# Expert rows that carry token number and residual: results scattered to token order, and a last stage that reads rows in order

## The chip, the cores and the metric

The kernel runs on one core of one Trainium2 chip. The metric is the device time of one execution in microseconds (us), as the median of several runs. The engines are named as in the profile: PE is TensorE (matrix products and transposes), DVE is VectorE, ACT is ScalarE, POOL is GpSimd, and SP is SyncE, which only issues DMAs here. A name with a q behind it (SPq, ACTq, POOLq) is an engine's own instruction queue. An indirect DMA takes the row addresses of one side from a column of integers in SBUF; POOL issues all of them.

## The reference, cut to what matters

The input is x, four images of 256 channels and 48 x 48 pixels, in float32. There are two layers. Each has a mixing part on the images and a feed-forward part (FFN) on tokens; a token is one pixel with its 256 channels. The change touches what happens from the end of layer 1's mixing part on.

```python
# layer 0: dynamic 7x7 attention, then an FFN on each image's 1151 tokens of highest router weight
x = x + attention0(_ln_c(x))
t = _to_tokens(x)
t = t + _L0_ffn_ref(_ln_t(t), ...)
x = _from_tokens(t, x)
# layer 1: four convolutions with weights of +-1, then a switch of 8 experts
x = x + convs1(_ln_c(x))
t = _to_tokens(x)
t = t + _L1_ffn_ref(_ln_t(t), ...)
x = _from_tokens(t, x)

def _L1_ffn_ref(h, gate_w, gate_b, w1, b1, w2, b2):     # T = 9216 tokens, E = 8 experts
    C = math.ceil(1.25 * T / E)                         # 1440 slots of each expert
    probs = softmax(x @ gate_w + gate_b)
    idx = argmax(probs);  prb = probs[idx]
    pos = cumulative count of idx's expert, in token order, minus 1
    kept = pos < C
    buf[idx, pos] = x                                   # tokens past the capacity are dropped
    ybuf = relu(buf @ w1 + b1) @ w2 + b2                # by expert
    y = ybuf[idx, min(pos, C - 1)] * (prb * kept)
    return nan_to_num(y, nan=0, posinf=10000, neginf=-10000)
```

Every token has at most one slot of one expert. The result of that slot, times the gate's probability, is added to the token's residual, which is t ahead of the layer norm. The output has the channels in front, so the last thing that the kernel does is to transpose tokens.

## The kernel before, in words

The kernel is written for a tile framework. A tile pool gives each named tile a number of buffers (`bufs`); an instruction that writes a tile waits until the former users of that buffer are done. The framework places each instruction on its engine's queue, and every queue runs in order. DMAs of SP and ACT share eight completion lanes and those of POOL have eight others; a DMA is issued only when the former DMA of its lane has landed.

There are four stages, and in the profile they follow one another with some overlap.

**Stage 1** (function body from line 162) is layer 0's attention. `conv` (L264) convolves four output rows of each of the four parity images with 49 taps, `attend` makes the softmax over the taps, which goes to DRAM in skewed form and back (`skew<-sp`, L313, and `at<-skew`, L315, both on SP), and `mix` adds the result and writes rows of tokens to the DRAM buffers `xl`. At its start ACT's queue issues 14 loads of the convolution's weights (L185). DVE and POOL make the batch norm's factors; one step is a power on POOL (L198). A tile of zeros (L218, L219) is written 40 times by SP (L383) over the whole of `xbuf`, so that empty slots of the experts read as zeros. `rank_count` counts, on DVE, how many tokens precede each one by router weight, and POOL scatters the token numbers by rank (`order<-ids`, L155).

**Stage 2** runs two things beside each other. `fetch` and `ffn` gather the chosen tokens' rows by indirect DMA (`g<-xl`, L454), apply layer 0's FFN and scatter the rows back (`xl<-y`, L492). The other is a software pipeline over 24 groups of 384 tokens (L640 to L657): `load` (`xt<-xl`) and norm, `to_channels`, `conv1` (L524), `to_tokens`, `gate` and `place`, each one step behind the former. `to_tokens` transposes the convolution's result back (L539), adds it to the residual, which stays in the resident tile `xt3` (L541), and writes the norm of it into a tile `row` of 128 x 3 x 260 with three buffers. `gate` puts the probability into column 256 of `row`. `place` works out each token's slot, keeps the slot in `gslot` and the mark of a kept token in `kept`, both resident, and scatters the three 128-row parts of `row` to their slots in the DRAM buffer `xbuf` (L618). Tokens without a slot get a number past the end and are not written.

**Stage 3** has 24 passes: eight experts with three passes each of 480 slots. `gather` loads the slots' rows from `xbuf` in one DMA (three buffers). `expert` transposes them (L695), makes the hidden layer (L702) and the output (L710), adds the bias and multiplies by the gate (L712, L713), applies nan_to_num to the whole tile (L721 to L724) and writes it to the same slots of the DRAM buffer `ybuf` (L725). ACT's queue loads the next expert's weights.

**Stage 4** has a loop over the same 24 groups. POOL gathers each 128 tokens' rows from `ybuf` by `gslot` (L757), DVE multiplies them by the mark and adds the residual of `xt3` (L760), PE transposes (L763), ACT and DVE copy the two halves of the channels (L766) into a tile `o` with two buffers, and SP writes it to the output (L768).

What the changed lines wait for can't be read from a loop alone. In stage 2 the buffer of `row` comes free when the three scatters of the group three steps back have landed. In stage 4 the gathers of `ybuf` wait for the last write of it.

Of the kernel before, what the change touches and what calls it, by code (L numbers as in the profile page):

```python
# [8 lines left out]
F32 = mybir.dt.float32  # L9
# [9 lines left out]
HW = H * W  # 2304 tokens of an image  # L19
NT = HW // P  # 18 tiles of 128 tokens  # L20
NG = 6  # groups of 8 image rows
GT = 384  # tokens of a group
KA = 49  # attention taps
SELK = 1151  # tokens that layer 0's FFN processes: top_k's first k - 1
NSEL = 9  # tiles of 128 ranks that hold them
E, CAP = 8, 1440  # experts, and the slots of each
FF = 1024
NF = FF // P
XROW = 260  # a row of the experts' buffer: 256 channels, the gate, padding
HOFF = [-4, -2, -1, 0, 1, 2, 4]  # offsets of layer 1's convolutions  # L30
FMAX = 3.4028234663852886e38

# One image, by row and column parity, is four 24x24 images in which the 7x7
# convolution and the attention have no dilation. They are padded to 30x30.
SP = 30
SRC = 10 * SP  # source pixels of four output rows
PITCH = 306  # a row of the attention matrix in DRAM; skewed writes use PITCH + 1
# [3 lines left out]
def metaformer_kernel(ctx: ExitStack, tc: tile.TileContext, i, out):  # L41
# [18 lines left out]
    # before[p, j] = j < p; after[p, j] = j > p; upto[p, j] = p <= j  # L60
# [13 lines left out]
    # 1 for every rank but the last of the ninth tile  # L74
# [3 lines left out]
    ids = const.tile([P, NT], I32, tag="ids", name="ids")  # L78
    nc.gpsimd.iota(ids, pattern=[[P, NT]], base=0, channel_multiplier=1)

# [14 lines left out]
    # rows of layer 0: [x + LN(x) | LN(x)], by image  # L95
    xl = [dram.tile([HW, 2 * C], F32, tag=f"xl{b}", name=f"xl{b}") for b in range(B)]
    # token of each rank, by image
    order = [dram.tile([HW, 1], I32, tag=f"order{b}", name=f"order{b}") for b in range(B)]
    xbuf = dram.tile([E * CAP, XROW], F32, tag="xbuf", name="xbuf")
    ybuf = dram.tile([E * CAP, C], F32, tag="ybuf", name="ybuf")  # L100

    def token_norm(work, src, dst, eps, np_=P):
        """dst = LN(src) over the free dim of [np_, 256]."""
# [9 lines left out]
    # Ranks of an image's router weights, ties by the lower token, are counted three tiles at  # L113
    # a time beside the next image's convolution.
# [4 lines left out]
    # the first tile has no earlier tokens, the last no later ones  # L119
# [42 lines left out]
    with ExitStack() as s1:  # L162
# [198 lines left out]
        for s in range(B * NG + 1):  # L361
# [20 lines left out]
            for k in range(2 * s, min(2 * s + 2, 40)):  # L382
                nc.sync.dma_start(zrows[k], zero)  # L383
# [10 lines left out]
    with ExitStack() as s2:  # L394
# [245 lines left out]
        for s in range(-1, len(groups) + 5):  # L640
# [3 lines left out]
            if c := now[0]:  # L644
                normed[c] = load(*c)
# [167 lines left out]
```

## Time and profile before

| What | Before |
|---|---|
| Median of three runs | 3820.05 us |
| Lowest and highest | 3817.47 and 3824.94 us |
| Span of the profiled execution | 3814.3 us |
| PE busy | 3545.5 us, 93% |
| DVE, ACT and POOL busy | 1211.3, 434.0 and 480.0 us |
| All DMA queues | 174.36 MB, 46 GB/s on average |
| Last expert result to the end of the span | 3708.0 to 3814.3, 106.3 us |

The span runs from the first to the last instruction that the profiler records in one execution, and the page gives no other time for that execution. The median of the runs shown is 5.75 us longer than the span.

A row of a group names the line, engine, operation and tiles (written<-read), then the number of instructions, the busy time, the mean time of one in nanoseconds, and the idle time of the engine ahead of them with what ended it. A row of waits has the engine, the instruction that waited, what it waited for, the sum, the number of waits and the longest. A row of DMA issues ends with the median time from issue to landing. In the rows of 40 slices each slice is 95.4 us long and a digit is the busy share in tenths; PEclk is the granted clock of TensorE in tenths. A row of the timeline has the start, the duration and the instruction, and in brackets how long its engine had been idle and what released it.

### The profile page before, as it was taken

The numbers are of one execution on the slowest core, as the hardware profiler recorded it, in microseconds if no ns is written. First come the engines' busy times: TensorE is split into PE (matmuls) and PEld (weight loads), VectorE is DVE, ScalarE is ACT, GpSimd is POOL, SyncE is SP. The second block draws the span as 40 slices with busy tenths as digits, with TensorE's granted clock in tenths as the row PEclk, the third lists the DMA queues.
The fourth block names the chain that finished last, engine by engine and source line by source line (L and its number), as shares of the span: only waits on it lengthen the run. The fifth ranks groups of instructions, "written<-read, shape, count | busy, mean of one in ns | idle before, by whom it ended". The sixth has DMA issues, their size and how long they took to land. (4 is left out here: it accounts for less than half of the span.)

```text
span 3814.3 us, 32485 instructions
## 1 busy us (share of the span) xinstructions
PE 3545.5 (93%) x12832; PEld 2248.8 (59%) x12832; DVE 1211.3 (32%) x3618; ACT 434.0 (11%) x779; POOL 480.0 (13%) x774
## 2 busy tenths in 40 slices
PE   6999999999999999999994789999999499999985
PEld 3566666666666666666663556666565366666652
DVE  3012124312235112261116312333443243333434
ACT  1001000000100000100001111211010022121211
POOL 1000001100001000020002322232332100000006
PEclk9999999999999999999996889999999699999995
DMA  7001100001100000110002221111000222222106
GB/s 231 13 25 39 36 25 25 25 25 35 40 25 25 25 25 27 34 27 21 21 21 76 62 63 31 41 34 44 18 17 18 80 61 59 59 62 66 49 27 193
DMA packets 122840, 174.36 MB, mean 46 GB/s; under 512 B 17089, under 2 KB 96193, under 8 KB 122689
## 3 DMA queue, kind: packets, MB, share of 16 engines
q1 hardware_dynamic: 92800, 111.41, 10.4%
q0 software_dynamic: 13824, 33.23, 2.9%
q10 hardware_dynamic: 16064, 27.66, 2.2%
q8 instruction: 100, 1.64, 0.2%
q14 instruction: 52, 0.42, 0.0%
HBM read 91.69 MB, written 80.58 MB: 45 GB/s over the span
## 5 line engine op out<-in xcount | busy, mean ns | idle before, releaser
L264 PE MATMUL c<-xp,cw 128*128 128x384 f32 x4704 | 1568.5, 492 | 0.9 <-DVE xp L256 0.9
L264 PEld LDWEIGHTS c<-xp,cw 128*128 128x128 f32 x4704 | 885.0, 189 | 663.0 <-issue 304.1
L524 PE MATMUL pc<-xq,cw 128*128 128x384 f32 x1344 | 467.1, 501 | 0.0
L329 DVE COPY av<-pa 120x192 f32<-120x192 f32 x96 | 32.0, 358 | 1096.9 <-PE pa L327 1096.9
L524 PEld LDWEIGHTS pc<-xq,cw 128*128 128x128 f32 x1344 | 254.8, 195 | 164.6 <-issue 12.8
L710 PE MATMUL pey<-ew,ehid 128*120 128x256 f32 x1536 | 335.4, 379 | 0.0
L702 PE MATMUL peh<-xeT,ew 128*128 128x480 f32 x768 | 316.5, 571 | 3.1 <-ACT xeT L697 3.1
L710 PEld LDWEIGHTS pey<-ew,ehid 128*120 128x120 f32 x1536 | 281.1, 183 | 59.2 <-issue 10.4
L109 POOL TENSOR_SCALAR bnrs<-bnmv 128x1 f32<-128x1 f32 x216 | 47.1, 223 | 1865.3 <-DVE bnmv L108 1864.0
L702 PEld LDWEIGHTS peh<-xeT,ew 128*128 128x128 f32 x768 | 145.0, 191 | 159.7 <-issue 151.0
L337 PE MATMUL pv<-av,xt 120*128 120x96 f32 (+1 forms) x1152 | 226.6, 329 | 0.0
L337 PEld LDWEIGHTS pv<-av,xt 120*128 120x128 f32 (+1 forms) x1152 | 181.8, 214 | 39.3 <-issue 11.4
L712 DVE TENSOR_TENSOR ey<-pey,eb 120x256 f32<-120x256 f32 x96 | 40.7, 424 | 431.1 <-PE pey L710 431.1
L269 ACT ACTIVATE k<-c,cb 128x384 f32<-128x384 f32 x24 | 14.0, 583 | 1323.4 <-PE c L264 1266.1
L757 POOL DMA_INDIRECT yt<-ybuf,gslot x72 | 69.9, 971 | 720.8 <-DMA ybuf<-ey 699.1
L704 ACT ACTIVATE ehid<-peh,eb 128x480 f32<-128x480 f32 x192 | 127.0, 662 | 294.6 <-PE peh L702 293.2
L480 PE MATMUL ph<-gt,fw 128*128 128x384 f32 x384 | 137.8, 520 | 6.2 <-ACT gt L475 5.8
L486 PE MATMUL py<-fw,hid 128*128 128x256 f32 x576 | 126.8, 379 | 3.0 <-DVE y L489 3.0
L110 POOL TENSOR_TENSOR bnrs<-bnrs,mhalf 128x1 f32<-128x1 f32 x216 | 125.0, 583 | 13.3
L486 PEld LDWEIGHTS py<-fw,hid 128*128 128x128 f32 x576 | 109.3, 190 | 21.1 <-DVE y L489 3.8
L480 PEld LDWEIGHTS ph<-gt,fw 128*128 128x128 f32 x384 | 76.7, 203 | 63.6 <-ACT gt L475 9.5
L763 PE MATMUL po<-ident,yt 128*128 128x128 f32 x144 | 50.8, 448 | 57.2 <-DVE yt L760 56.1
(169 smaller groups left out, 2599.3 us busy)
## 6 DMA issues: line engine op xcount, KB each, us to landing
xl<-rows SPq DMA_DIRECT2D x24, 768.0 KB, 3.5
ew<-in_L_ffn_w_dram ACTq DMA_DIRECT2D x16, 1024.0 KB, 5.4
skew<-sp SPq DMA_DIRECT2D x24, 575.6 KB, 4.3
at<-skew SPq DMA_DIRECT2D x24, 562.5 KB, 4.8
xbuf<-zero SPq DMA_DIRECT2D x40, 292.5 KB, 7.8
xe<-xbuf SPq DMA_DIRECT2D x24, 487.5 KB, 4.5
ybuf<-ey SPq DMA_DIRECT2D x24, 480.0 KB, 3.6
x<-in_x_dram SPq DMA_DIRECT2D x24, 384.0 KB, 3.4
```

The source lines that it names most:

```text
L109: nc.gpsimd.tensor_scalar_add(rs[:np_], mv[:np_, 1:2], eps)
L110: nc.gpsimd.tensor_tensor(rs[:np_], rs[:np_], mhalf[:np_, 0:1], ALU.pow)
L264: nc.tensor.matmul(ps, lhsT=cw1[:, cc, t, :], rhs=xp[:, cc, :, 4 * g + ki:4 * g + ki + 4, kj:kj + 24], start=(t == 0 and cc == 0), stop=(t ...
L337: nc.tensor.matmul(pv[:, q], lhsT=xts[b, g + k][:n, q, cc * P:(cc + 1) * P], rhs=av[:n, q, k], start=(k == 0), stop=(k == 2))
L480: nc.tensor.matmul(ph, lhsT=fw1[:, cc, f * P:(f + 1) * P], rhs=gt[:, cc], start=(cc == 0), stop=(cc == 1))
L486: nc.tensor.matmul(py, lhsT=hid[:, f, k * P:(k + 1) * P], rhs=fw2[:, f], start=(f == 0), stop=(f == NF - 1))
L524: nc.tensor.matmul(ps, lhsT=cws[n][:, cc, t], rhs=xq[:, cc, 4 + 8 * g + dy:12 + 8 * g + dy, 4 + dx:4 + dx + W], start=(t == 0 and cc == 0) ...
L702: nc.tensor.matmul(ph, lhsT=w1[:, cc, f * P:(f + 1) * P], rhs=xeT[:, cc], start=(cc == 0), stop=(cc == 1))
L704: nc.scalar.activation(hid[:, f], ph, AF.Relu, bias=eb1[:, e * NF + f:e * NF + f + 1])
L710: nc.tensor.matmul(py[:R], lhsT=hid[:, f, j * R:(j + 1) * R], rhs=w2[:, f], start=(f == 0), stop=(f == NF - 1))
L757: nc.gpsimd.indirect_dma_start(out=y, out_offset=None, in_=ybuf, in_offset=bass.IndirectOffsetOnAxis(ap=gslot[b][:, n:n + 1], axis=0))
L763: nc.tensor.transpose(pts[cc][:, k * P:(k + 1) * P], y[:, cc * P:(cc + 1) * P], ident)
```

## The change

A row of `xbuf` becomes 516 elements wide: 256 of the norm, the gate, the token's number as an integer, two of padding, and 256 of the residual. `ybuf`, `xt3`, `gslot` and the resident `kept` go. A new DRAM buffer `fin` has one row of 256 for each token.

- In stage 1 the zero tile covers two rows of 516 per partition; its token column holds `NONE`, a number past the end. It is written 45 times.
- In stage 2 the residual's tile is a work tile `x` with five buffers. `to_tokens` adds the convolution and the residual into the last 256 columns of `row`, writes the token numbers with a POOL copy, and SP writes the residual of all 384 tokens to their rows of `fin`. `place` loses two small DVE operations.
- In stage 3 each of the four 120-row parts of a pass gets its residual added on DVE, and is scattered by POOL to the token rows of `fin`. Empty slots carry `NONE` and are not written. The order of the DMAs on `fin` is kept by the framework.
- In stage 4 ACT's queue loads the 384 rows of a group from `fin` in order; there is no gather and no addition. The loop over the halves of the channels is now outside that over the three parts, and `o` has three buffers.

```diff
-XROW = 260  # a row of the experts' buffer: 256 channels, the gate, padding
+XHEAD = 260
+XROW = XHEAD + C
+NONE = 1 << 30
...
-    ids = const.tile([P, NT], I32, tag="ids", name="ids")
+    ids = const.tile([P, B * NT], I32, tag="ids", name="ids")
...
-    ybuf = dram.tile([E * CAP, C], F32, tag="ybuf", name="ybuf")
+    fin = dram.tile([B * HW, C], F32, tag="fin", name="fin")
...
-        zero = wpool.tile([P, 585], F32, tag="zero", name="zero")
-        nc.gpsimd.memset(zero, 0.0)
-        zrows = xbuf.rearrange("n r -> (n r)").rearrange("(k p r) -> k p r", p=P, r=585)
+        zero = wpool.tile([P, 2, XROW], F32, tag="zero", name="zero")
+        nc.gpsimd.memset(zero.rearrange("p j r -> p (j r)"), 0.0)
+        nc.gpsimd.memset(zero[:, :, C + 1:C + 2].bitcast(I32), NONE)
+        zrows = xbuf.rearrange("(k p j) r -> k p j r", p=P, j=2)
...
-            for k in range(2 * s, min(2 * s + 2, 40)):
+            for k in range(2 * s, min(2 * s + 2, 45)):
                 nc.sync.dma_start(zrows[k], zero)
-    xpool = pool("xtok", 1)
-    xt3 = [xpool.tile([P, NT, C], F32, tag=f"xt3_{b}", name=f"xt3_{b}") for b in range(B)]
-    gslot = [xpool.tile([P, NT], I32, tag=f"gslot{b}", name=f"gslot{b}") for b in range(B)]
-    kept = [xpool.tile([P, NT], F32, tag=f"kept{b}", name=f"kept{b}") for b in range(B)]
...
-            x = xt3[b][:, 3 * g:3 * g + 3]
+            x = work.tile([P, 3, C], F32, tag="x", name=f"x1_{b}_{g}", bufs=5)
...
-            x = xt3[b][:, 3 * g:3 * g + 3]
             row = work.tile([P, 3, XROW], F32, tag="row", name=f"row{b}_{g}", bufs=3)
-            nc.gpsimd.memset(row[:, :, C + 1:], 0.0)
+            nc.gpsimd.memset(row[:, :, C + 2:XHEAD], 0.0)
+            nc.gpsimd.tensor_copy(
+                row[:, :, C + 1].bitcast(I32), ids[:, b * NT + 3 * g:b * NT + 3 * g + 3])
...
-                nc.vector.tensor_add(x[:, k], pt, x[:, k])
-                token_norm(work, x[:, k], row[:, k, :C], 1e-5)
+                xk = row[:, k, XHEAD:]
+                nc.vector.tensor_add(xk, pt, x[:, k])
+                token_norm(work, xk, row[:, k, :C], 1e-5)
+            n0 = b * HW + g * GT
+            nc.sync.dma_start(fin[n0:n0 + GT, :].rearrange("(k p) c -> p k c", p=P),
+                              row[:, :, XHEAD:])
...
-            nc.vector.tensor_scalar_min(slot, pos, CAP - 1.0)
-            nc.vector.tensor_add(slot, slot, ex)
-            nc.vector.tensor_copy(gslot[b][:, 3 * g:3 * g + 3], slot)
+            nc.vector.tensor_add(slot, pos, ex)
...
-            nc.sync.dma_start(ybuf[n0:n0 + N, :].rearrange("(j p) c -> p j c", p=R), y)
+            for j in range(J):
+                nc.vector.tensor_add(y[:, j], y[:, j], xe[:, j, XHEAD:])
+                nc.gpsimd.indirect_dma_start(
+                    out=fin,
+                    out_offset=bass.IndirectOffsetOnAxis(
+                        ap=xe[:, j, C + 1:C + 2].bitcast(I32), axis=0),
+                    in_=y[:, j], in_offset=None, bounds_check=B * HW - 1, oob_is_err=False)
...
-                o = work.tile([P, 2, GT], F32, tag="o", name=f"o{b}_{g}")
-                pts = [ps_t.tile([P, GT], F32, tag="t", name=f"po{b}_{g}_{cc}")
-                       for cc in range(2)]
-                for k in range(3):
-                    n = 3 * g + k
-                    y = work.tile([P, C], F32, tag="y", name=f"yt{b}_{n}", bufs=8)
-                    nc.gpsimd.indirect_dma_start(
-                        out=y, out_offset=None, in_=ybuf,
-                        in_offset=bass.IndirectOffsetOnAxis(ap=gslot[b][:, n:n + 1], axis=0))
-                    nc.vector.scalar_tensor_tensor(y, y, kept[b][:, n:n + 1], xt3[b][:, n],
-                                                   ALU.mult, ALU.add)
-                    for cc in range(2):
-                        nc.tensor.transpose(pts[cc][:, k * P:(k + 1) * P],
-                                            y[:, cc * P:(cc + 1) * P], ident)
+                n0 = b * HW + g * GT
+                y = work.tile([P, 3, C], F32, tag="y", name=f"yt{b}_{g}", bufs=8)
+                nc.scalar.dma_start(y, fin[n0:n0 + GT, :].rearrange("(k p) c -> p k c", p=P))
+                o = work.tile([P, 2, GT], F32, tag="o", name=f"o{b}_{g}", bufs=3)
                 for cc in range(2):
-                    (nc.vector.tensor_copy if cc else nc.scalar.copy)(o[:, cc], pts[cc])
+                    pt = ps_t.tile([P, GT], F32, tag="t", name=f"po{b}_{g}_{cc}")
+                    for k in range(3):
+                        nc.tensor.transpose(pt[:, k * P:(k + 1) * P],
+                                            y[:, k, cc * P:(cc + 1) * P], ident)
+                    (nc.vector.tensor_copy if cc else nc.scalar.copy)(o[:, cc], pt)
```

The diff leaves out removed comments, and lines whose only change is that `x` is handed from `load` to `to_tokens`.

## The prediction

> **What bounds the kernel now.** First the page's busy shares, its slices and the windows of the last two stages.
>
> ```profile
> PE 3545.5 (93%) x12832; PEld 2248.8 (59%) x12832; DVE 1211.3 (32%) x3618; ACT 434.0 (11%) x779; POOL 480.0 (13%) x774
> ...
> PE   6999999999999999999994789999999499999985
> ...
> DMA  7001100001100000110002221111000222222106
> ...
> 3015.00:3708.00 693.00, 668.44 (x2496) 447.97 (x2496) 247.30 (x360) 140.46 (x216) 0.00 (x0) 0.99 0.20 53
> 3735.00:3785.00 50.00, 27.48 (x78) 13.19 (x78) 24.07 (x52) 6.05 (x13) 37.87 (x40) 0.50 0.65 199
> ```
>
> TensorE is the bound nearly throughout. Only slice 1, slices 22 and 23 (layer 0 to layer 1), slice 32 (experts start) and the last slice and a half fall short, and only there can the change gain. The expert window (columns: length, then PE, PEld, DVE, ACT, POOL busy, clock, DMA share, GB/s) has PE at 668 of 693 us, DVE at 36% and POOL at nothing. The final stage has PE half idle at clock 0.50 and DMA at 0.65.
>
> Next the final stage's groups, waits and timeline.
>
> ```profile
> L757 POOL DMA_INDIRECT yt<-ybuf,gslot x72 | 69.9, 971 | 720.8 <-DMA ybuf<-ey 699.1
> ...
> ACT o L766 <- DMA out_dram<-o: 56.2, 16, 4.8
> DVE yt L760 <- DMA yt<-ybuf,gslot: 54.8, 53, 7.2
> ...
> 3708.01 0.32 SPq L725 DMA_DIRECT2D ybuf<-ey  x1
> 3712.41 0.99 POOL L757 DMA_INDIRECT yt<-ybuf,gslot  x1 [699.06 <-DMA ybuf<-ey]
> 3713.70 0.97 POOL L757 DMA_INDIRECT yt<-ybuf,gslot  x1 [0.30 <-issue]
> ```
>
> Gathers start every 1.27 us (0.97 plus 0.30 of gap), three to a group: 24 x 3 x 1.27 = 91 us from 3712.4 to 3803.9, then 10 us of tail. That issue rate sets the last 106 us (3708.0 to 3814.3).
>
> **The change, part by part** (against the span of 3814.3; the median of the runs shown, 3820.05, is 5.75 above it, and I add the same 5.75).
>
> *Final stage.* 72 gathers and 72 DVE additions go (91 us of POOL, 35 of DVE); 24 loads of 384 KB on ACT's queue come.
> Entry: the last block of nan_to_num ends at 3708.0. Before, the ybuf write landed 3.55 later and the first gather issued at 3712.41. Now one addition (0.42, by the 120x256 row of L712) and four indirect scatters follow, each waiting for the one before, because all write `fin`; 120 rows of 1 KB. Nearest rows: a scatter of 1040 B rows repeats every 2.77 us (2806.46 to 2809.23), the layer-0 scatter of 1 KB rows about every 3.2. At 2.9: 0.42 + 4 x 2.9 = 12.0, so 3720. First load by the 6.4/3.4 of the 384 KB rows below: 5.5, so 3725.5.
> Pitch per group: three limits. PE: six transposes of 0.447 at half clock, 2.1 overlapped. DMA: 18.9 MB in and out; this trace moves about 300 GB/s when its share is full (199/0.65 = 306), so 63 us, 2.6 per group. Loop: ACT issues load i only after its copy of group i-3 (three `o` buffers, one in-order queue), so (6.4 + 0.4 + 2.1 + 0.55)/3 = 3.1. I take 2.9; bounds 2.6 and 3.6 (loads at 8.3, the slowest xt<-xl).
> The Trainium skill (DMA: Bandwidth & Descriptors, Measured) gives 425 GB/s for a 16 MB load, and its section on where 436 comes from about 358 for HBM per core: 18.9 MB would take 44 to 53 us, pitch 1.9 to 2.2, PE-bound. The row mixes loads and stores in 1 KB packets as this stage does, so it decides; by the page the gain is 16 us more.
> End: 3725.5 + 23 x 2.9 + 2.1 + 0.55 + 3.3 (out) = 3798. **-16** (-23 to 0).
>
> ```profile
> xbuf<-zero SPq DMA_DIRECT2D x40, 292.5 KB, 7.8
> xe<-xbuf SPq DMA_DIRECT2D x24, 487.5 KB, 4.5
> xt<-xl SPq DMA_DIRECT2D x24, 384.0 KB, 6.4
> order<-ids,rki POOLq DMA_INDIRECT x72, 2.1
> xbuf<-row,si POOLq DMA_INDIRECT x72, 2.6
> xl<-y,idx POOLq DMA_INDIRECT x36, 2.4
> ...
> 2809.23 0.97 POOL L618 DMA_INDIRECT xbuf<-row,si  x1 [1.79 <-DMA xbuf<-row,si]
> 2811.81 0.11 POOL L535 MEMSET row<- 128x9 f32 x1 [1.61 <-DMA xbuf<-row,si]
> 2812.27 0.76 DVE L541 TENSOR_TENSOR xt<-pcv,xt 128x256 f32<-128x256 f32 x2 [8.98 <-PE pcv L539]
> ...
> 34.22 1.28 ACT L240 ACT_TABLE_LOAD   x1 [34.22 <-DMA cw<-in_L_conv_w_dram]
> ```
>
> *Wider scatters.* 72 scatters go from 1040 to 2064 B rows. Landing rises from 2.1 (4 B) to 2.6 (1040 B), 0.5 per KB, but the 1 KB rows of layer 0 land in 2.4, 0.3 per KB. The same page's fit (Anatomy of one DMA), 2.0 us plus bytes at 436 GB/s, makes 0.30 for 131 KB more. I take 0.35: 3.1 per scatter; bounds 0.2 and 0.75 (a write of twice the bytes amid fuller queues).
>
> *Stage 2 loop.* Before, the addition writes `xt`, which nobody else holds; only the memset waits for the row slot's last scatters (2811.81), 0.46 ahead of the addition. Now the addition writes the row itself, so it waits too, and behind it on DVE stand the norm, the gate's arithmetic and the slot cast that releases the next scatters: a loop of 14.1 (addition to cast, from 2789.0 to 2803.13) and three scatters. Two slot operations fewer save 0.2-0.3. Three wider scatters cost 1.05; less 0.46 of slack and 0.2, +0.4 to +0.75 in each of some seven steps without an FFN: +3.5. In the three steps behind an FFN step the addition ran ahead of the memset (2431.9 against 2433.3, 2500.2 against 2503.9, 2574.0 against 2575.8), so it loses 1.4 to 3.6 and the wider scatters' 1.05; PE has convolutions of the next group (9 us each) over half of it: 1.5 x 3 = 4.5. In steps with an FFN PE is full, nothing. The ids copy and memset on POOL (0.1 to 0.3) stand behind the same wait. The 24 `fin<-row` writes of 384 KB (9.4 MB) stand on SP ahead of the next step's loads, which come a step early: hidden, at 0.1-0.2 of DMA share; without that cover up to 3.4 a step. **+8** (+3 to +18).
>
> *Drain into the experts.* After the last conv, twelve scatters run serially (2971.4 to 3014.9), two under the expert weights' loads at 7.2 and about 6. All PE waits. 12 x 0.35 = +4.2, less 2 for the last groups' scatters that can start while their predecessors' norms end. Against the change speaks the same page's Latency section: HBM answers in 0.2 us on average and 2 at high load. Did the added `fin<-row` writes make load enough, each scatter would cost 1.8 more, 21 in all; but only the two under 1 MB weight loads show such a delay, and no `fin` write is larger than 384 KB. **+2** (-3 to +8).
>
> *First expert load.* 4.70 us for 487 KB at 3015.0; 968 KB at 300 GB/s adds 1.6, with latency under load **+2** (1.7 to 3). The other 23 loads are a pass (28.3 us) early: hidden.
>
> *Expert stage.* Four additions (4 x 0.42 = 1.7 us) and four scatters (some 12 us) per pass of 28.3: DVE has 64% free, POOL all; `ey` has two buffers, `xe` three. **0** (0 to +4); without cover it would be 24 x 12.
>
> *Start.* 45 zero writes of 516 KB replace 40 of 292.5 (23.8 for 12.0 MB). Their tile's second memset stands on POOL behind the 8.2 us power of the batch norm (22.4 to 30.7), so zeros begin near 31, not 24. ACT's first square waits at 34.22: the last of 14 weight loads was held by a completion lane that a zero write had. With zeros later it waits for an earlier weight load and is free near 29: conv starts 4.5 sooner. Zeros at 300 GB/s then run to about 113; SP's next DMA, the first skew, is at 128.8, so 15 us cover remains; without it the first attend slips. **-4.5** (-6 to +2).
>
> *Layer 0 to 1.* 74 KB a partition of resident tokens, slots and marks vanish, so FFN weights and first row fetches can load before stage 1's memory is free; PE idles about 64 us around 2050-2250, but DVE's rank counting (48 of 50 us) sets most. **-3** (-8 to +4).
>
> Sum: -16 + 8 + 2 + 2 + 0 - 4.5 - 3 = -11.5: span 3802.8, time **3808.5**.
>
> **Rivals.**
> *A, slower: the stage-2 loop takes over.* Scatters at 3.5 or more instead of 3.1 (the +0.75 end): three cost 2.25 a step; minus 0.66, 1.6 x 7 = 11, and 3.3 x 3 = 10 behind FFN steps, 21; drain 12 x 0.75 - 2 = 7; entry of the final stage 2 more. Against -23.5 of start, transition and final stage, +2 for `xe`: 21 + 7 + 2 + 2 - 23.5 = +8.5, **3828.5**. It decides from about 3.3 per scatter. For: every scatter is serial and the addition's slack is 0.46. Against: 1 KB and 4 B rows differ by only 0.3.
> *B, the final stage stays where it was.* Pitch 3.6 because loads and stores queue on each other: 3725.5 + 83 + 6 = 3814, gain 0: +4.5, **3824.5**. For: outs already held ACT 56 us. Against: two `o` buffers then, three now.
> *C, larger gain.* Pitch 2.6, stage 2 hidden under PE (+3), drain 0: -23 + 3 + 0 + 2 - 5 - 6 = -29, **3791**. For: PE is the bound in stage 2.
>
> That the gathers stay is excluded: their instructions are gone.
>
> **How the numbers follow.** Mine 0.50, A 0.20, B 0.12, C 0.18. 0.2% (7.6 us) is about what a measurement tells from no change. Within mine (own range 3798 to 3819) faster is 0.72, same 0.23, slower 0.05; A: 0, 0.3, 0.7; B: 0.1, 0.6, 0.3; C: 1. Faster 0.36 + 0.01 + 0.18 = 0.55, rounded to 0.56; same 0.25 rounded to 0.23; slower 0.21. Leaving out the outer tenth of A and of C gives 3788 to 3831.
>
> **What would show it.** Final stage: no POOL; first load near 3720 of the old clock, groups every 2.9, and PE still near half clock. Wrong if the pitch is over 3.5. Stage 2: the addition released by DMA xbuf<-row; step 23.3 growing to about 24. Wrong if scatters land beyond 3.2. First square near 29 to 30; first skew not later than the convolution. Expert passes stay at 28.3; wrong if PE waits on `xe` or DVE on `ey`. Drain: 48 to 55 us from the first of its twelve scatters to the first expert transpose (48.4 before, 2971.4 to 3019.7).

## The result and the profile after

The changed kernel takes 3793.95 us in the median of four runs (3791.75 to 3797.50), the kernel before on the same chip 3822.49 us (3817.47 to 3834.97, four runs). The ratio is 0.9923 with a 95% interval of 0.9905 to 0.9940: 0.77% faster, 28.5 us. The profiled execution took 3792.99 us and has a span of 3790.7, so it is compared with the span of 3814.3 before: 23.6 us less. I had forecast 3808.5 us, 11.5 less, with a range of 3788 to 3831. Direction and range were right; the gain is more than twice what the sum said.

These are the page's rows of the changed kernel that answer to those shown of before: engines, then slices of PE and DMA.

```profile
PE 3516.3 (93%) x12832; PEld 2242.8 (59%) x12832; DVE 1209.4 (32%) x3594; ACT 433.1 (11%) x779; POOL 515.3 (14%) x823
...
PE   6999999999999999999995779999999399999995
...
DMA  9001100001100001100002111121111422322316
```

TensorE bounds the kernel as before. DMA is busier at the start (zero writes of twice the bytes), in the experts' stage and at the end. The windows of the experts' stage and of the last stage (columns as before):

```profile
3015.00:3708.00 693.00, 665.07 (x2474) 445.05 (x2475) 272.13 (x442) 140.16 (x216) 98.61 (x93) 0.98 0.28 68
3735.00:3785.00 50.00, 30.24 (x138) 23.84 (x138) 12.42 (x23) 11.00 (x23) 0.00 (x0) 0.60 1.03 355
```

POOL now works 98.6 us among the experts, and not at all in the last stage, where DMA is full: share 1.03, 355 GB/s, in place of 0.65 and 199. To see where the 23.6 us come from, I cut each trace at its first and last matrix products (the start times of the first and last matmul of each group), so that each stage can be compared alone:

| Stage, from and to | Before | After | Difference | Forecast |
|---|---|---|---|---|
| start: to the first layer-0 convolution | 44.9 | 40.9 | -4.0 | -4.5 |
| layer 0: first to last convolution matmul | 1942.2 | 1937.1 | -5.1 | 0 |
| transition: to the first layer-1 convolution | 297.9 | 295.8 | -2.1 | -3 |
| layer 1: first to last convolution matmul | 670.6 | 677.0 | +6.4 | +8 |
| drain and first expert load: to the first expert transpose | 64.1 | 75.0 | +10.9 | +4 |
| experts: to the last output product | 680.2 | 686.8 | +6.6 | 0 |
| end: last output product to the end of the span | 114.4 | 78.1 | -36.3 | -16 |

So three terms were right (start, transition, layer 1), two costs were too low (drain and experts), layer 0 had no term, and the last stage gained more than twice what I had put. Each column is one execution: a later trace of the same changed kernel has 682.3 us for the experts in place of 686.8, and the other stages behind layer 0 within 4.0 us (see below). The timeline of the changed kernel there, from the residual additions of the last pass on:

```profile
3720.75 1.43 DVE L729 TENSOR_TENSOR ey<-ey,xe 120x256 f32<-120x256 f32 x4
3721.47 1.25 POOL L730 DMA_INDIRECT fin<-ey,xe  x1 [15.95 <-DVE ey L729]
3725.19 1.00 POOL L730 DMA_INDIRECT fin<-ey,xe  x1 [2.47 <-DMA fin<-ey,xe]
3728.41 1.00 POOL L730 DMA_INDIRECT fin<-ey,xe  x1 [2.23 <-DMA fin<-ey,xe]
3731.35 1.00 POOL L730 DMA_INDIRECT fin<-ey,xe  x1 [1.93 <-DMA fin<-ey,xe]
3733.51 2.00 ACTq L762 DMA_DIRECT2D yt<-fin  x4
3736.86 2.82 PE L767 MATMUL po<-ident,yt 128*128 128x128 f32 x12 [23.86 <-DMA yt<-fin]
```

The four scatters are serial, each released by the landing of the one before, and cost 12.8 us between the end of nan_to_num (3720.72) and the first load (3733.51). The first load is used 3.35 us later. The last transpose starts at 3786.2, so 23 groups follow the first at (3786.2 - 3736.9)/23 = 2.14 us each.

### The profile page after: what moved, and what is told of

The parts are those of the page before. It is cut to its first block, busy times and chain, and to the rows that moved or that the text cites. A ratio compares the mean times of both kernels' runs of the same rounds, so it can differ in the third digit from the quotient of the medians.

```text
span 3790.7 us, 32733 instructions
## 1 busy us (share of the span) xinstructions
PE 3516.3 (93%) x12832; PEld 2242.8 (59%) x12832; DVE 1209.4 (32%) x3594; ACT 433.1 (11%) x779; POOL 515.3 (14%) x823
## 5 line engine op out<-in xcount | busy, mean ns | idle before, releaser
L524 PE MATMUL pc<-xq,cw 128*128 128x384 f32 x1344 | 458.4, 494 | 0.0
L713 PEld LDWEIGHTS pey<-ew,ehid 128*120 128x120 f32 x1536 | 281.1, 183 | 59.2 <-issue 10.4
L730 POOL DMA_INDIRECT fin<-ey,xe x96 | 101.9, 1061 | 614.0 <-DVE ey L729 429.8
L621 POOL DMA_INDIRECT xbuf<-row,si x72 | 73.1, 1016 | 211.0 <-DMA xbuf<-row,si 113.3
```

Source lines behind the costliest of these rows:

```text
L524: nc.tensor.matmul(ps, lhsT=cws[n][:, cc, t], rhs=xq[:, cc, 4 + 8 * g + dy:12 + 8 * g + dy, 4 + dx:4 + dx + W], start=(t == 0 and cc == 0) ...
L621: nc.gpsimd.indirect_dma_start(out=xbuf, out_offset=bass.IndirectOffsetOnAxis(ap=si[:, k:k + 1], axis=0), in_=row[:, k], in_offset=None, b ...
L713: nc.tensor.matmul(py[:R], lhsT=hid[:, f, j * R:(j + 1) * R], rhs=w2[:, f], start=(f == 0), stop=(f == NF - 1))
L730: nc.gpsimd.indirect_dma_start(out=fin, out_offset=bass.IndirectOffsetOnAxis(ap=xe[:, j, C + 1:C + 2].bitcast(I32), axis=0), in_=y[:, j], ...
```

## The experiments

My theory after the traces: the end gained because loads in order run at the DMA's rate; the wide rows cost in the layer-1 stage and the drain; and `xe` buffers, held until the scatters land, cost in the experts. The rivals are told with each run. Chips differ, and so do executions, so each time is given as a ratio to the kernel before on the same chip, with the stage lengths beside it.

### Four buffers of xe

```diff
-            xe = work.tile([R, J, XROW], F32, tag="xe", name=f"xe{e}_{q}", bufs=3)
+            xe = work.tile([R, J, XROW], F32, tag="xe", name=f"xe{e}_{q}", bufs=4)
```

> The changed kernel with four buffers of xe in place of three. Theory: an xe buffer is now held until the last of its pass's four scatters has landed, so the load for two passes on starts late, and PE waits for it at the start of an expert; then the waits of PE for xe after the first one (10.2 us in five) fall below 2 us, first expert transpose to last output product shrinks from 686.8 to about 680.5 us, and the time is 6 us shorter, near 3788. Rival: the load of 968 KB is itself late, since it shares the DMA engines with the scatters and the weights; then another buffer changes nothing, within 2 us of the changed kernel.

Measured: 3790.03 us, ratio 0.9933 (0.9910 to 0.9956); the expert stage took 681.3 us. PE's waits between 3015 and 3690 us, first in the changed kernel:

```profile
PE pe L698 <- DMA xe<-xbuf: 44.7, 6, 34.5
PE pe L698 <- DVE ey L727: 2.7, 1, 2.7
```

And with four buffers:

```profile
PE pe L698 <- DMA xe<-xbuf: 36.9, 2, 33.9
PE pe L698 <- DVE xeT L700: 8.3, 6, 1.4
```

And in the kernel before, behind its drain:

```profile
PE pe L695 <- DVE xeT L697: 9.0, 7, 1.4
```

The longest wait for `xe` in each is the drain, which is ahead of the experts. Behind it 10.2 us in five waits fell to 3.0 in one, for the second load right behind the first, and the old wait for the transposed copy came back. What the loads of `xe` wait for changed as the theory says; SyncE's waits between 3040 and 3700 us, before and after:

```profile
SPq L685 <- DVE ey L713: 449.6, 21, 37.4
SPq L688 <- DMA fin<-ey,xe: 619.6, 42, 59.6
```

So the theory holds for the waits, but not for its 6 us. The first trace of the changed kernel also has the wait of 2.7 us above and a half-clock interval of 3.4 us among the experts; the three other traces with three wide buffers and the same passes have neither, and their stages are 682.3, 683.5 and 683.6 us long. PE's idle time in the stage (its length less PE's busy time) is 11.7 us before, 15.1 to 16.7 in these four traces, and 13.7 to 13.8 in the three with four wide buffers (681.2 to 682.4 us). A fourth buffer is worth 1 to 3 us, too little for the whole time to show.

### Five buffers of row

```diff
-            row = work.tile([P, 3, XROW], F32, tag="row", name=f"row{b}_{g}", bufs=3)
+            row = work.tile([P, 3, XROW], F32, tag="row", name=f"row{b}_{g}", bufs=5)
```

> The changed kernel with five buffers of row in place of three. Theory: the addition that writes the row waits for the scatters of three groups before; with five buffers it waits for those of five groups before, so DVE's waits for xbuf<-row (87.5 us in nine) vanish and the way from the first to the last layer-1 convolution shrinks from 677.0 to about 670.6 us as before the change; the time is 6 us shorter, near 3788, or more if the drain starts earlier. Rival: POOL's serial scatters set the pace, and the addition only shows them; then the wait moves to the slots or to POOL, and the time stays within 2 us of the changed kernel.

Measured: 3787.11 us, ratio 0.9934 (0.9918 to 0.9951); layer-1 stage 677.2 us, drain 76.1: no gain in time. The wait on the row is gone, as the timeline shows for one addition of the changed kernel and then for one of this run:

```profile
2809.60 0.10 POOL L534 MEMSET row<- 128x6 f32 x1 [1.94 <-PE pcv L540]
2809.68 0.76 DVE L543 TENSOR_TENSOR row<-pcv,x 128x256 f32<-128x256 f32 x2 [9.69 <-DMA xbuf<-row,si]
```

```profile
2813.64 0.75 DVE L543 TENSOR_TENSOR row<-pcv,x 128x256 f32<-128x256 f32 x2 [9.25 <-PE pcv L540]
2814.28 0.10 POOL L534 MEMSET row<- 128x6 f32 x1 [2.25 <-PE pl L564]
```

The releaser is again PE's transpose. From one convolution block to the next, most steps behind the last FFN are 23.3 or 24.9 us long in this run and in the kernel before, and 23.7 to 24.6 in the changed kernel, so the new wait does cost 0.7 us in a tight step. But the steps around the FFNs became longer here (the fifth to the tenth, from the ninth product of a block to that of the next: 25.0, 45.0, 29.9, 46.3, 30.2 and 47.3 us, against 23.3, 45.0, 26.0, 46.1, 26.1 and 45.9 before), and in the drain the slot cast waited 13.7 us for the scatters instead, since the tile of slots has two buffers. PE's waits between 2050 and 2960 us, two rows of the changed kernel and then one of this run, which has no wait for the addition:

```profile
PE pcv L540 <- DVE row L543: 17.8, 14, 5.0
PE pgate L570 <- DVE lt L566: 14.9, 20, 0.8
PE pgate L570 <- DVE lt L566: 24.1, 22, 5.6
```

So half of the wait moved, to the gate, as the rival has it. The other half did go: PE's idle time in the layer-1 stage is 17.8 us before, 34.0 in the changed kernel and 25.3 here. But this execution has 34.1 us of half clock in the stage in place of 20.5, and PE's busy time is 8.9 us longer. Whether the half clock came of the moved waits or by chance, one trace can't tell.

### Narrow rows, all waits kept

```diff
-    xbuf = dram.tile([E * CAP, XROW], F32, tag="xbuf", name="xbuf")
+    xbuf = dram.tile([E * CAP, XHEAD], F32, tag="xbuf", name="xbuf")
...
-                    in_=row[:, k], in_offset=None, bounds_check=E * CAP - 1, oob_is_err=False)
+                    in_=row[:, k, :XHEAD], in_offset=None, bounds_check=E * CAP - 1, oob_is_err=False)
...
-                nc.vector.tensor_add(y[:, j], y[:, j], xe[:, j, XHEAD:])
+                nc.vector.tensor_add(y[:, j], y[:, j], xe[:, j, :C])
```

(The residual is left out of `xbuf`, and the experts add the norm in its place. The zero tile and `xe` are narrow too.)

> The changed kernel with every wait and every DMA kept, but rows of xbuf 260 wide again: the residual is not scattered into xbuf (it is left out; the experts add the norm in its place), so scatters move 1040 B rows, zero writes 260 KB and expert loads 487 KB. It tells bytes from waits. If the bytes cost: scatters of xbuf repeat every 2.8 us in place of 3.3, the drain (first of the last twelve scatters to first expert transpose, 59.2 us) falls to about 53, the first load by 2.5, stage 2 by 3 to 5, PE's waits for xe by 8: 15 us shorter, 3779. If the waits cost and the bytes do not: only the first load's 2.5 us, 3791.

Measured: 3782.62 us, ratio 0.9929 (0.9912 to 0.9946). Layer-1 stage 670.5 us, drain 68.8, experts 678.9: 6.5, 6.2 and 7.9 less than in the changed kernel. DMA issues of the changed kernel, then of this one (last column: median us from issue to landing):

```profile
xe<-xbuf SPq DMA_DIRECT2D x24, 967.5 KB, 7.2
xbuf<-row,si POOLq DMA_INDIRECT x72, 3.0
```

```profile
xe<-xbuf SPq DMA_DIRECT2D x24, 487.5 KB, 4.5
xbuf<-row,si POOLq DMA_INDIRECT x72, 2.6
```

The bytes cost, not the added waits alone: with 1040 B rows PE's idle time in the layer-1 stage is 20.9 us, against 34.0 with wide rows and 17.8 before, although the addition still writes the row. The stage is back at its 670.6 us; in the two later kernels with narrow rows it is 673.2 and 672.5, so 2 to 3 us can remain. In tight steps width and wait cost only together, since either alone leaves them at 23.3 us; around the FFNs wide rows cost even without the wait. Among the experts PE has no wait for `xe` any more, though three buffers are still held until the scatters land: the hold costs only together with the 7.2 us of a wide load.

In the drain 4.7 us remain over the kernel before with narrow rows. About half of them lie between the seventh and the ninth of the last twelve scatters, which run beside loads of 1 MB of weights; these three before, and then in the changed kernel:

```profile
2994.30 0.97 POOL L618 DMA_INDIRECT xbuf<-row,si  x1 [6.99 <-DVE si L616]
3000.51 0.97 POOL L618 DMA_INDIRECT xbuf<-row,si  x1 [5.24 <-DMA xbuf<-row,si]
3003.25 0.97 POOL L618 DMA_INDIRECT xbuf<-row,si  x1 [1.77 <-DMA xbuf<-row,si]
```

```profile
2992.76 0.97 POOL L621 DMA_INDIRECT xbuf<-row,si  x1 [7.55 <-DVE u L607]
3000.80 0.97 POOL L621 DMA_INDIRECT xbuf<-row,si  x1 [7.07 <-DMA xbuf<-row,si]
3005.22 0.97 POOL L621 DMA_INDIRECT xbuf<-row,si  x1 [3.46 <-DMA xbuf<-row,si]
```

From the first to the third it is 9.0 us before, 12.5 in the changed kernel and 11.2 here. Why these come later beside the same loads wasn't tried.

### nan_to_num and scatters by parts in every pass

The block of nan_to_num, the addition and the scatter move into the loop over the four parts of a pass:

```diff
             for j in range(J):
...
+                    nc.vector.copy_predicated(yj, bad, fill[:R].to_broadcast([R, C]))
+                nc.vector.tensor_add(yj, yj, xe[:, j, XHEAD:])
+                nc.gpsimd.indirect_dma_start(
```

> The changed kernel with nan_to_num, residual addition and scatter done for each 120-row part as soon as its products are there, in place of once for the whole pass. Theory: the serial scatters of the last pass (12.8 us) and the block of nan_to_num (7 us) lie bare ahead of the final stage; by parts three quarters of both lie under PE, so last output product to first load of the final stage shrinks from 20.9 to about 8 us, and xe buffers come free some 5 us earlier in each pass, so 2 to 4 us of PE's waits for xe go too: 14 to 17 us shorter, 3777 to 3780. Rival: 24 small DVE instructions a pass in place of 6 delay the copies of xeT that PE waits for; then passes grow by 0.5 us or more (12 us in all) and half or more of the gain is lost, 3786 or above.

Measured: 3803.52 us (20 runs), ratio 0.9978 (0.9968 to 0.9987). The last output product to the first load did shrink from 20.9 to 8.2 us, but the experts took 711.1 us in place of 686.8. PE's waits between 3050 and 3690 us:

```profile
PE pe L698 <- DVE xeT L700: 14.1, 6, 2.4
PE peh L705 <- DVE xeT L700: 11.9, 16, 1.0
```

Together 26 us, all for DVE's half of the transposed copy, which stands on DVE behind the small instructions of the former pass's last part. PE's idle time in the stage is 32.3 us in place of 16.7, and there are four half-clock intervals of 3.4 us in place of one. The rival is right, and costs more than the theory gains.

### By parts in the last pass alone

```diff
+                if (e, q) == todo[-1]:
+                    finish(e, q, xe, y, j, j + 1)
+            if (e, q) != todo[-1]:
+                finish(e, q, xe, y, 0, J)
```

with four buffers of `xe` (`finish` holds nan_to_num, addition and scatters for the parts j to j + 1, or for all four).

> The changed kernel with four buffers of xe, and with nan_to_num, addition and scatter by 120-row parts in the last of the 24 passes alone. Theory: small DVE instructions hurt only where a next pass's copies of xeT stand behind them on DVE, and behind the last pass none do; so last output product to first load falls from 20.9 to about 8 us with the passes at 681 us in all as with four buffers: 18 us less than the changed kernel, ratio to the kernel before 0.988. Rival: the scatters of the pass before still fill POOL when the last pass's parts are ready, and the entry stays above 14.

Measured: 3775.53 us, ratio 0.9903 (0.9887 to 0.9920). Last output product to first load is 8.3 us, experts 682.1. The theory holds in both stages; the ratio of 0.988 that it named is just outside the interval. The same kernel ran again beside the last ones below:

> The changed kernel with four xe buffers and the last pass by parts (wide rows, plain scatters), again, on the chip of the other two. Theory: 16 to 18 us less than the changed kernel on this chip: experts 681 to 682 in place of 684 to 687, last output product to the end 67.5 in place of 78 to 80; ratio 0.987 to 0.990.

Measured: 3773.69 us, ratio 0.9910 (0.9885 to 0.9934); experts 682.4, last output product to the end 64.3.

### What bounds the last stage: half of the bytes in

```diff
-                nc.scalar.dma_start(y, fin[n0:n0 + GT, :].rearrange("(k p) c -> p k c", p=P))
+                nc.scalar.dma_start(y, fin[n0:n0 + GT, :P].rearrange("(k p) c -> p k c", p=P))
...
-                                            y[:, k, cc * P:(cc + 1) * P], ident)
+                                            y[:, k], ident)
```

> The changed kernel whose last stage loads only the first 128 channels of each row (192 KB a group) and transposes them twice; the other half of the output's channels is left out. It tells what sets the pitch of the last stage, 2.1 us a group with DMA share at 1.03 and 355 GB/s. If the bytes do: 192 + 384 KB at 355 GB/s are 1.66 us a group, so first load to the end shrinks from 57.2 to 46 to 48 us. If the loop of three buffers and ACT's in-order queue does (load, transposes, copy), the pitch stays above 1.95 and the stage above 53.

Measured, in one execution: first load to the end 44.5 us in place of 57.2, with a pitch of (3770.3 - 3733.6)/23 = 1.60 us. The window over its last stage, with nearly the same transposes:

```profile
3731.00:3775.00 44.00, 24.36 (x144) 19.10 (x144) 13.38 (x24) 11.48 (x24) 0.00 (x0) 0.84 0.96 322
```

A quarter fewer bytes, a quarter less pitch, well under the 1.95 us that the loop of buffers and ACT's queue would have kept: the bytes bind, and not the loop.

### Loads in order, and nothing else of the change

```diff
-                    y = work.tile([P, C], F32, tag="y", name=f"yt{b}_{n}", bufs=8)
-                    nc.gpsimd.indirect_dma_start(
-                        out=y, out_offset=None, in_=ybuf,
-                        in_offset=bass.IndirectOffsetOnAxis(ap=gslot[b][:, n:n + 1], axis=0))
+                y3 = work.tile([P, 3, C], F32, tag="y", name=f"yt{b}_{g}", bufs=3)
+                nc.scalar.dma_start(y3, ybuf[n0:n0 + GT, :].rearrange("(k p) c -> p k c", p=P))
```

> The kernel before, where only the last stage's 72 gathers are replaced by 24 loads on ACT's queue that read rows of ybuf in slot order, and o has three buffers; the additions of the resident residual stay, and the permutation of rows is left out. It measures what the last stage gains by loads alone, without any of the change's costs. Theory (the gathers' issue rate was the bound, and 355 GB/s is the next): last output product to first load 12 us as before, first load to the end 57 in place of 102, so 44 us less than the kernel before, ratio 0.988 to 0.989. Rival (the stage gained because DVE's additions went too): DVE with 2.0 us a group or the wait of loads on additions keeps the pitch at 2.6 or more, and the gain is 33 us or less.

Measured: 3768.75 us, ratio 0.9892 (0.9875 to 0.9908). Last output product to the end is 70.1 us in place of 114.4, a gain of 44.3, which the theory had named. Its two parts were not as named. The loads read the first 9216 slots, which the last pass doesn't write, so they started at 3683.4, before the last output product (3696.7); and from the first transpose (3705.3) to the end it took 61.5 us, against 53.9 in the changed kernel:

```profile
3725.00:3760.00 35.00, 23.69 (x84) 13.03 (x84) 24.45 (x58) 6.71 (x14) 0.00 (x0) 0.50 0.95 312
```

DVE is busy for 24.45 of 35 us there, in place of 12.42 of 50, and DMA at 0.95. So the loads make the gain: from the first transpose to the end 37.1 us (98.6 before), where the changed kernel gains 44.7. The other 7.2 of the 44.3 come of the early start, which a kernel that must wait for the last pass can't have, so that the sum met the theory is luck. The 7.6 us between the two last stages go with the additions that left DVE, or with this kernel's three buffers for the loaded rows; that wasn't parted.

### Narrow rows that still carry the residual: scatters that add

`fin` has every token's residual already, so the experts' scatters can add to it in the DMA, and rows of 260 suffice (with four buffers of `xe`, and the last pass by parts):

```diff
-                nc.vector.tensor_add(y[:, j], y[:, j], xe[:, j, XHEAD:])
...
-                    in_=y[:, j], in_offset=None, bounds_check=B * HW - 1, oob_is_err=False)
+                    in_=y[:, j], in_offset=None, bounds_check=B * HW - 1, oob_is_err=False,
+                    compute_op=ALU.add)
```

> As the one with the last pass by parts and four xe buffers, but rows of xbuf are 260 wide again and carry norm, gate and token number; the residual lies in fin already, and the experts' scatters add to it in the DMA (an accumulating write) in place of DVE's addition. Theory (the wide rows cost 6.5 us in stage 2, 6.2 in the drain, the rest in the loads): first to last layer-1 convolution 671 us, drain 69, experts 679 to 680, so 12 to 16 us less than with wide rows, ratio to the kernel before 0.984. Rival: an accumulating scatter [...]takes 5 us or more where a plain one takes 3.2; then four of them no longer fit beside the output products of the last pass, entry 12 or more, and passes wait for ey.

Measured: 3776.64 us, ratio 0.9917 (0.9888 to 0.9946), not the forecast 0.984. Layer-1 stage 673.2 (forecast 671), drain 67.9, experts 679.8: about as the theory has it. But the entry to the last stage is 13.6 us (3696.2 to 3709.8):

```profile
3694.23 1.60 POOL L735 DMA_INDIRECT fin<-ey,xe  x1 [3.03 <-DVE ey L716]
3698.91 1.60 POOL L735 DMA_INDIRECT fin<-ey,xe  x1 [3.09 <-DVE bad_AluOpType.is_lt L732]
3703.51 1.60 POOL L735 DMA_INDIRECT fin<-ey,xe  x1 [3.00 <-DMA fin<-ey,xe]
3707.06 1.60 POOL L735 DMA_INDIRECT fin<-ey,xe  x1 [1.95 <-DMA fin<-ey,xe]
```

In the median an adding scatter repeats every 4.2 us and a plain one every 3.5, and a part's output products take 3.5; the first two steps here are 4.7 and 4.6. So the four no longer fit beside the output products, as the rival has it, and its 12 us or more came true; passes that wait for `ey`, its other sign, did not come. Why an adding scatter takes longer isn't shown. The next kernel takes plain scatters for the last pass, whose residual rows POOL gathers two passes early:

```diff
+                if last:
+                    nc.vector.tensor_add(y[:, j], y[:, j], rests[j])
...
+            if n + 2 == len(todo):
+                residuals(nxt)
```

> As the kernel with narrow rows and accumulating scatters, except the last pass: its residual rows are gathered from fin two passes early, added on DVE, and the scatters are plain ones. Theory: the entry to the last stage was 13.6 us there since an accumulating scatter repeats every 4.6 us, longer than the 3.5 us of a part's output products; plain ones at 3.3 make it 8 to 9 us, so last output product to the end 67 us as with wide rows by parts; with layer-1 stage 671 to 673, drain 68 and experts 680 this is 8 us less than the wide-row version by parts and 18 to 24 less than the changed kernel, ratio 0.986 to 0.988. Rival: the four gathers stand on POOL ahead of the scatters of the pass before and hold them, and the last pass's scatters start behind 8 of others: entry 12 us or more.

Measured: 3768.65 us (3766.63 to 3777.10), ratio 0.9900 (0.9876 to 0.9924). Entry 9.8 us, layer-1 stage 672.5, drain 68.9, experts 679.6, last output product to the end 67.6: each near its forecast, but the whole gained less against the kernel before than I had put, and this run can't tell it from the wide rows with the last pass by parts.

### The changed kernel again, and the half clock in layer 0

> The changed kernel itself, beside the next two on one chip. Theory: the ratio to the kernel before is 0.991 to 0.994 again. Its executions differ by some 10 us through the number of TensorE's half-clock intervals in layer 0's convolutions, which no edit here touches; if so, the difference of the convolution stage between two kernels (first to last matmul) goes with half of the half-clock time, and the other stages repeat within 3 us: transition 292 to 296, layer-1 stage 677 to 680, drain 74 to 76, experts 683 to 687, last output product to the end 78 to 80.

Measured: 3789.80 us (3770.68 to 3806.45, nine runs), ratio 0.9952 (0.9924 to 0.9980): 18.3 us less than before on this chip. The medians of the two best kernels, both with the last pass by parts (wide rows, and narrow rows with plain scatters last), lie 16.1 and 21.2 us lower on this chip; the intervals of their ratios overlap or meet this one. Transition 291.8, drain 74.7, layer-1 676.4, experts 682.3 and end 77.6 are within 4.5 us of the first trace, but layer 0 took 1928.6 us in place of 1937.1, with 85.3 us at half clock in place of 99.0. Over all fourteen traces this stage ranges from 1928.6 us (85.3 at half clock) to 1951.6 (136.5): 23 us for 51, a little under half a microsecond for each. It accounts for the 5.1 us that I hadn't forecast: 116.1 us at half clock before, 99.0 after, worth up to 8.5. The windows show it (column ahead of the DMA share: granted clock); first before, then after:

```profile
460.00:540.00 80.00, 79.94 (x281) 49.55 (x280) 12.80 (x35) 6.54 (x12) 2.38 (x6) 0.96 0.10 27
540.00:620.00 80.00, 79.94 (x280) 49.34 (x279) 16.67 (x42) 6.24 (x13) 0.00 (x0) 0.97 0.09 25
```

```profile
460.00:540.00 80.00, 79.94 (x290) 48.83 (x289) 15.31 (x45) 6.63 (x13) 2.37 (x6) 1.00 0.11 30
540.00:620.00 80.00, 79.80 (x304) 49.34 (x303) 18.93 (x45) 6.77 (x14) 2.37 (x6) 1.00 0.09 27
```

### Zeros late in the kernel before

```diff
         nc.gpsimd.memset(zero, 0.0)
+        nc.gpsimd.memset(zero[:, 256:258], 0.0)
```

> The kernel before with a second memset of two columns of the zero tile, which POOL does behind the batch norm's power, so that the writes of zeros begin behind it as in the changed kernel, at half their bytes. Theory: the first convolution stands behind ACT's last weight load, which is held by a completion lane that a zero write has; with zeros late it is 3 to 5 us sooner: 17 to 18.7 us behind the start of the power in place of 21.2 to 22.5. Rival: the earlier start of the changed kernel comes of the zero writes' size or of the other added instructions; then 21 or more.

This didn't do what it was for: the zero writes still began at 20.92 us, right behind the start of the power at 20.44, and the first convolution came 22.0 us behind the latter. It is one execution (3827.33 us), and inconclusive by itself. The other kernels answered, because the order on POOL differed among them without my doing. Where zeros began ahead of the power's end (the kernel before, with loads in order, this one, and the narrow rows), the first convolution stood 20.1 to 22.5 us behind the power's start; where they began behind it (all with wide rows), 16.3 to 18.5. The completion lanes, each a semaphore in the traces, show why. In the six traces of the first group the last DMA on the lane of ACT's last weight load is a zero write, and the load is issued 0.02 to 0.03 us after that has landed (33.85 after 33.83 in the kernel before). In the eight of the second it is an earlier weight load, which lands sooner (26.52 after 26.50 in a later trace of the changed kernel). So it is the order that moves the start. Whether the size of the writes matters too isn't parted: all of 260 and 292.5 KB began early, and all of 516 KB late.

## Why the prediction was right, and where its sum was off

- **Start, -4.5.** Right (-4.0), and as the mechanism has it, ACT's first instruction moved from 34.22 to 30.25, behind the last weight load, which is issued at 29.88 in place of 33.85. Its completion lane was held by a zero write before, and by an earlier weight load after (see the zeros above).
- **Layer 0.** I had no term for it. The half clock gave 5.1 us, and gives it or takes it in any execution.
- **Layer 0 to 1, -3.** Right in size (-2.1). What carried it wasn't tried.
- **Stage 2 loop, +8.** The mechanism "the addition writes the row itself, so it waits too" is right; the size (+6.4) is in part luck. PE's idle time in the stage rose by 16.2 us (17.8 to 34.0), and its busy time fell by 9.7 (652.7 to 643.0), about half of it by 10.2 us less at half clock. Tight steps grew from 23.3 to about 24, as the last part of the prediction had it, and in more steps than seven; but the steps of 24.9 us, which hold a half-clock interval, nearly vanished there (nine intervals, 30.7 us, before; four, 20.5, after), so little of it was left. The loss came in the steps around the FFNs: the first ten steps are 6.4 us longer, the others together not at all. Wide scatters were +0.4 (2.6 to 3.0 us to landing), where I took 0.35.
- **Drain, +2, and first load, +2.** The load is right: 7.2 us in place of 4.7. The drain was mis-sized: with 10.9 for both, it cost 8.4, and its twelve scatters took 52.1 us in place of 43.6. Two steps failed. One is "less 2 for the last groups' scatters that can start": the last group's addition waited 6.7 us for its row (before, the norm behind it had waited 5.1), so nothing started sooner. The other is 0.35 for each of the twelve: the two that follow the seventh came 3.5 us later than before (see the narrow rows), and the others 0.5 each.
- **Expert stage, 0 (0 to +4).** The failed step is "`ey` has two buffers, `xe` three". I counted buffers, and not who holds them. The scatter reads its row addresses from `xe` and the addition reads the residual from it, so a buffer comes free only when the fourth scatter has landed, not when the gate has been multiplied. So the claim that "the other 23 loads" are hidden fails where PE takes half of the next pass's transposes a pass early, once an expert: there it waited for a load of 7.2 us that started late, four times, 7.2 us in all (the fifth wait stays with four buffers). The stage was +6.6 in the first trace, 2.2 to 3.5 in the three others with three wide buffers, and a fourth buffer takes 1 to 3 of it away.
- **Final stage, -16.** The mechanism is right, its pitch was mis-sized: 2.14 us in place of 2.9, that is 17.5 us over 23 groups, and 2 more for the first load (3.35 in place of 5.5). The entry was right (12.8 for 12.0). The failed step is "the row mixes loads and stores in 1 KB packets as this stage does, so it decides". 199 GB/s at a share of 0.65 made 306 GB/s, but the full share turned out to be 355. The Trainium skill's 358 GB/s of HBM for a core (DMA: Bandwidth & Descriptors, on where 436 comes from) was within 1%; why it fits mixed loads and stores isn't shown here. Its 2.2 us a group would have made -32 for the stage and 3792 for the whole, close to the measured time by chance, since other terms were off too. PE wasn't in the way: six transposes took 0.84 to 1.54 us where the loads came in bursts, less than the 2.1 that I took from a stage in which each pair waited.

The rivals: A (the stage-2 loop takes over) is excluded: stage 2 lost 6.4 us and not 21, with scatters at 3.0 to landing. B (the end stays) is excluded by the pitch. C has the right total (3791) and the larger gain of the end, but neither the hidden stage 2 nor the free drain that it named. The sum was wrong by +7 and +7 in two costs and by -20 and -5 in two gains; that these offset one another is luck. Two of the signs of being wrong came true: PE waited on `xe`, and the drain from its first scatter to the first expert transpose took 59.2 us, not 48 to 55.

## What to carry to other kernels

A scatter that takes its addresses or data from a tile is a reader of that tile until it lands: count it among the holders of the buffer before calling a prefetch hidden. A small DMA in a serial chain costs its landing time per link (here 2.7 us to landing, and a link every 2.9 to 3.7), so look at what the chain stands ahead of; splitting it pays where nothing is behind it on the splitting engine, here the last pass only. A rate scaled up from a window where DMA is not full is a guess from below: run one where it is full before it decides over a gain. And a stage's length in one trace mixes waits with the clock that was granted: part PE's idle time from its busy time, and look at a second trace of the same kernel, before a few microseconds are given to an edit.

## What the runs showed of the hardware

In layer 0 the granted clock fell to half in intervals of 3.41, 6.83 and 10.24 us. In all fourteen traces each of the 11 to 16 intervals began in, or right behind, the small products of the attention's mix (`pv<-av,xt`, 96 columns wide), while PE was idle for 2.2 to 2.9 us in the whole stage and never for more than 0.80 at once; so the profile shows no idle gap that would set them off. How much of it there was differed from execution to execution: nine of the changed kernel on one chip took 3770.68 us at a mean granted clock of 0.949 to 3806.45 at 0.940. The Trainium skill (TensorE: Matmul & The Clock Gate, on the clock gate) has free-running windows of 3.4 us, and the lengths are multiples of that; that the phase of the windows decides which products are caught is argued and wasn't tried. It moves layer 0 by up to 23 us here, as much as the change itself. And an accumulating indirect scatter of 120 rows of 1 KB held POOL for 1.60 us in place of 1.00 and landed in 3.9 us in place of 2.7.
